# Last image: variance of the residual sum from a covariance gathered in the last attention, and residual sums made inside the q, k, v loop

## The chip, the cores and the metric

The kernel runs on one core of one Trainium2 chip. The metric is the device time of the whole program in microseconds (us): the median of several executions.

## The reference, cut to what matters

Four images of 256 channels and 64x64 pixels go through four residual layers. `N` is 4096 pixels; the 256 channels are held as two halves (`h` = 0, 1) of 128 partitions.

```
# layer 0: x + f(gn32(x)); f: 3x3 convolution, group norm, relu -> xs; then non-local attention on xs
f    = einsum('bnc,bcm->bnm', theta(xs), phi(xs))
attn = softmax(f, axis=-1)
y    = einsum('bnm,bmc->bnc', attn, g(xs))
w_y  = group_norm(conv1x1(y, w_w, w_b), gn2_w, gn2_b)
x    = x + (w_y * 0.1 + xs)
# layer 1: x + linear attention on gn(x); _gn takes mean and variance of groups of 8 channels
qkv  = einsum('oc,bchw->bohw', w_qkv, rmsnorm(gn(x)))
q, k = softmax over 32 channels, softmax over pixels
out  = rmsnorm(w_out @ (context(k, v) applied to q))
# layer 2: depthwise 3x3 and pointwise products with generated filters; layer 3: mixture of four 1x1 filters
```

Between layers 0 and 1 the kernel needs, for each channel, mean and variance over the pixels of the *residual sum* r = sc * wy + xin (+ a shift), where wy is the 1x1 convolution of the attention's result, sc its group-norm scale (known only when wy is complete), and xin the sum of x and xs.

## The kernel before, in words

Everything is fp32. The order of the instructions of each engine is that of the code (`manual_schedule`): a chain of generators (`Chain.steps`) is stepped together with the generator `attend`, and each `yield n` of the chain adds n times a rate to a credit; a whole unit of credit gives one turn to the attention. So while the attention of image b runs, the tail of image b-1 (`nonlocal_out`, `linear_attention`, `generated`, `mixed`) and the convolution of image b+1 fill the other engines. Images count from 0; the last is image 3, with `diag` and `xs_in` given in its tail. Its attention runs with the tail of image 2 beside it (rate 1.24) and then alone; its own tail runs after it, with nothing beside it except 16 pieces of image 2's last product, held back in `held`: `fill(n)` issues the matmuls of n pieces (4 matmuls of 512 columns each), `settle` drains them on VectorE and stores them.

- `attend(b)` (L888): 8 blocks `q` of 512 columns, each of 16 iterations `m`. An iteration makes two logits products (pf, L898), their exponentials on ScalarE (pr, L899), two products with g (py, L937), and adds pr into tot on VectorE. `ended` (L902) finishes a block in five stages, during the next block's first iterations: the sum inv (L906) at m=15; pss at m=0; the reciprocal and yt at m=1; ps_wy and its copies to wt (L922) at m=2; the statistics of wt (bn_stats, L925) and its store to DRAM (wy_d, L926) at m=3.
- `residual_sums` (L956): 16 passes of ScalarE over the last image's xin (`x_cols`), with a running sum, in the last block or so of the last attention. They give the mean of xin.
- `nonlocal_out` (L966): for the last image it loads wy six parts ahead (parts of 1024 columns and one half), closes the statistics of wy (`group_finish`, L330), makes sc and sh (`affine`, L365), adds sc * wy + xin into `big` in eight instructions of VectorE (L127), squares each around the known mean on ScalarE (L1014), and sums the squares (L1000, L1001).
- `group_finish`: a matmul pm averages the means over a group, VectorE makes ev, a matmul pv averages that, VectorE adds eps (rstd, L354), and POOL takes the power -1/2 (L217).
- `linear_attention` (L1023): `normed(c)` writes 512 columns, normalised, to xg (L1033) and their squares to sq (L1035) on ScalarE, and VectorE adds the halves of sq (s2; the profile calls it s). For each c: `normed(c+1)`; `qkv(c)`, 16 matmuls ps_qkv (L1057) with their evictions to qk (L1061) and v (L1062); the norms of c+1 (ps_ss, L1043, and rinv, L1045); `context(c-1)` (ps_qt, ps_ctx).
- Helpers: VectorE's `tt` is L124, `stt` L127.

Buffers: tiles of 4 KB a partition (pr, tot, wt, wy, xs, xg, sq, qk, v, z, dw, wp2, ex) share nine of one tag, `k4`; a new tile waits for the last reader of the one that had its place. The last tail takes every second of its tiles from four spare ones (`in_turns`), whose names in the profile are ra and rt.[...]

```python
def k4(name):
    return wk.tile([P, CH], F32, tag="k4", name=name, bufs=9)
```

Of the kernel before, what the change touches and what calls it, by code (L numbers as in the profile page):

```python
# [13 lines left out]
P = 128  # L14
# [79 lines left out]
def conv_preact_fast(ctx: ExitStack, tc: tile.TileContext, guard, x, wc, wtpg, ww, wqkv, wout, w1cat, wd2,  # L94
# [235 lines left out]
    def group_finish(st, avg, eps, shift=None):  # L330


        if callable(st):
            mv = st()
        else:
            mv = sp.tile([P, NH, 2], F32, name="mv")
            for h in range(NH):
                nc.vector.bn_aggr(mv[:, h, :], st[:, h, :, :].rearrange("p c s -> p (c s)"))
        if shift is not None:
            tt(mv[:, :, 0], mv[:, :, 0], shift, ALU.add)  # L340
        yield 1
        pm = bank("pm")
        nc.tensor.matmul(pm[:, 0:NH], avg, mv[:, :, 0], start=True, stop=True)
        gm = sp.tile([P, NH], F32, name="gm")
        nc.vector.tensor_copy(gm, pm[:, 0:NH])
        ev = sp.tile([P, NH], F32, name="ev")
        tt(ev, mv[:, :, 0], gm, ALU.subtract)
        tt(ev, ev, ev, ALU.mult)
        tt(ev, ev, mv[:, :, 1], ALU.add)
        yield 1  # L350
        pv = bank("pv")
        nc.tensor.matmul(pv[:, 0:NH], avg, ev, start=True, stop=True)
        rstd = sp.tile([P, NH], F32, name="rstd")
        nc.vector.tensor_scalar(rstd, pv[:, 0:NH], eps, None, ALU.add)  # L354
        rsqrt(rstd, rstd)
        return mv, gm, rstd
# [530 lines left out]

    def attend(b):  # L888

        probs, todo = {}, []  # L890
        st = wy_stats[b] = sp.tile([P, NH, 8, 6], F32, name="wy_st")

        def logits(i):
            q, m = divmod(i, NM)
            pr = k4("pr")
            for s in range(2):
                pf = bank("pf")
                nc.tensor.matmul(pf, phi[:, bass.ts(2 * m + s, P)], theta[:, bass.ts(q, 512)], start=True, stop=True)  # L898
                nc.scalar.activation(pr[:, bass.ts(s, 512)], pf, AF.Exp)  # L899
            probs[i] = pr  # L900

        def ended(q, py, tot):  # L902

            at = b * NQ + q
            inv = wk.tile([P, 512], F32, tag="inv", name="inv")
            nc.vector.scalar_tensor_tensor(inv, tot[:, 0:512], 1.0, tot[:, 512:CH], ALU.mult, ALU.add,  # L906
                                           accum_out=guard[:, 0, at:at + 1])
            yield
            pss = bank("pss")
            nc.tensor.matmul(pss, ones, inv, start=True, stop=True)  # L910
            yield
            nc.vector.reciprocal(inv, pss)  # L912
            yt = k2("yt")
            tt(yt, py, inv, ALU.mult)
            yield
            nc.scalar.activation(junk(), inv, AF.Copy, accum_out=guard[:, 1, at:at + 1])

            wt = k4("wt").rearrange("p (h n) -> p h n", h=NH)
            for h in range(NH):
                ps = bank("ps_wy")  # L920
                nc.tensor.matmul(ps, ww_s[:, bass.ts(h, P)], yt, start=True, stop=True)  # L921
                nc.scalar.copy(wt[:, h, :], ps)  # L922
            yield
            for h in range(NH):
                nc.vector.bn_stats(st[:, h, q, :], wt[:, h, :])  # L925
            nc.sync.dma_start(out=wy_d[b].rearrange("h p n -> p h n")[:, :, bass.ts(q, 512)], in_=wt)  # L926

        logits(0)
        for i in range(NQ * NM):
            q, m = divmod(i, NM)  # L930
            if m == 0:
                py = bank("py")
                tot = k4("tot")
            if i + 1 < NQ * NM:
                logits(i + 1)
            for s in range(2):
                nc.tensor.matmul(py, g[:, bass.ts(2 * m + s, P)], probs[i][:, bass.ts(s, 512)],  # L937
                                 start=(m == 0 and s == 0), stop=(m == NM - 1 and s == 1))
            if m == 1:
                tt(tot, probs[i - 1], probs[i], ALU.add)  # L940
            elif m > 1:
                tt(tot, tot, probs[i], ALU.add)
            for t in todo:
                next(t, None)
            if m == NM - 1:
                todo = [ended(q, py, tot)]
                next(todo[0])
            yield i + 1 < NQ * NM
        for t in todo:
            for _ in t:  # L950
                yield


    res_sum = cp.tile([P, NH], F32, name="res_sum")

    def residual_sums(xs_in):  # L956

        parts = sp.tile([P, NH, N // 512], F32, name="res_parts", bufs=1)
        for h in range(NH):
            for c in range(N // 512):  # L960
                nc.scalar.activation(junk(), xs_in[:, h, bass.ts(c, 512)], AF.Copy, accum_out=parts[:, h, c:c + 1])
                yield
        nc.vector.tensor_reduce(res_sum, parts, AX.X, ALU.add)


    def nonlocal_out(w, b, big, k4, xs_in):  # L966
# [4 lines left out]
        def load_parts(i):  # L971
            c, h = PARTS[i]
            wy = k4("wy")
# [7 lines left out]
        ahead = 2 if xs_in is None else 6  # L981
        parts = [load_parts(i) for i in range(ahead)]
        if xs_in is not None:
            yield 1
        bias = vec_s[:, V_WB, :]
        wmv, gm, rstd = yield from group_finish(wy_stats[b], avg32, 1e-5, bias)
        sc, sh = affine(gm, rstd, vec_s[:, V_G2W, :], vec_s[:, V_G2B, :], bias, 0.1)
        st = stats_tile()
        if xs_in is not None:

            mv = sp.tile([P, NH, 2], F32, name="mv_in", bufs=1)
            centre = sp.tile([P, NH], F32, name="centre", bufs=1)
            squares = sp.tile([P, NH, N // CH], F32, name="squares", bufs=1)
            tt(mv[:, :, 0], wmv[:, :, 0], bias, ALU.subtract)
            tt(mv[:, :, 0], mv[:, :, 0], sc, ALU.mult)
            stt(mv[:, :, 0], res_sum, 1.0 / N, mv[:, :, 0], ALU.mult, ALU.add)
            nc.vector.tensor_scalar(centre, mv[:, :, 0], -1.0, None, ALU.mult)

            def moments():
                nc.vector.tensor_reduce(mv[:, :, 1], squares, AX.X, ALU.add)  # L1000
                nc.vector.tensor_scalar(mv[:, :, 1], mv[:, :, 1], 1.0 / N, None, ALU.mult)  # L1001
                return mv

            st = moments
        w.fill(2)
        for i, (c, h) in enumerate(PARTS):
            cols = bass.ts(c, CH)
            wy, xs = parts[i]
            stt(big[:, h, cols], wy, sc[:, h:h + 1], xs, ALU.mult, ALU.add)
            if i + ahead < len(PARTS):  # L1010
                parts.append(load_parts(i + ahead))
            yield 0.6
            if xs_in is not None:
                nc.scalar.activation(wy, big[:, h, cols], AF.Square, bias=centre[:, h:h + 1], accum_out=squares[:, h, c:c + 1])  # L1014
            else:
                for s in range(2):
                    nc.vector.bn_stats(st[:, h, 2 * c + s, :], big[:, h, bass.ts(2 * c + s, 512)])
            yield 0.6
        w.settle()
        return st, sh  # L1020


    def linear_attention(w, b, big, qT, k4, st, sh, alone):  # L1023
        _, gm, rstd = yield from group_finish(st, avg8, 1e-5, sh)
# [56 lines left out]

        ahead = normed(0)
        yield 1
        ready = *ahead, None
        last = None
        for c in range(NC):
            if c + 1 < NC:
                ahead = normed(c + 1)
# [10 lines left out]
        rk = sp.tile([P, 1], F32, name="rk")  # L1099
# [98 lines left out]
    def generated(w, b, big, k4, st, sh, diag):  # L1198
        mv, gm, rstd = yield from group_finish(st, avg8, 1e-5, sh)

        pivot = sp.tile([P, NH], F32, name="pivot")
# [7 lines left out]
        hs = sp.tile([HT * HP, NC3], F32, name="hs")  # L1209
# [6 lines left out]
        b1n = sp.tile([HT * HP, 1], F32, name="b1n")  # L1216
# [33 lines left out]
        pooled = sp.tile([HT * HP, 1], F32, name="pooled")  # L1250
        nc.vector.tensor_reduce(pooled, hs, AX.X, ALU.add)
        pd = sp.tile([HT * HP, 2 * R], F32, name="pd")
# [5 lines left out]
        pb = sp.tile([P, 2 * R], F32, name="pb")  # L1258
# [3 lines left out]
        dk = sp.tile([P, NH * 9], F32, name="dk")  # L1262
# [118 lines left out]
        sh2 = sp.tile([P, NH], F32, name="sh2")  # L1381
# [4 lines left out]
    def mixed(w, b, big, k4, st, sh, held):  # L1386
# [7 lines left out]
        pool = sp.tile([P, NH], F32, name="rpool")  # L1394
# [6 lines left out]
        hid = sp.tile([EH, 1], F32, name="hid")  # L1401
# [6 lines left out]
        nm = sp.tile([P, 1], F32, name="lnm")  # L1408
        nc.vector.tensor_reduce(nm, pl[:, 0:NE], AX.X, ALU.max, negate=True)
        al = sp.tile([P, NE], F32, name="al")  # L1410
        asum = sp.tile([P, 1], F32, name="asum")
# [5 lines left out]
        scales = sp.tile([P, NH, NE], F32, name="scales")  # L1417
# [15 lines left out]
        b3 = sp.tile([P, NH], F32, name="b3")  # L1433
# [46 lines left out]
    def tail(b, big, qT, k4=k4, diag=None, xs_in=None, held=None):  # L1480

        def layers(w):
            st, sh = yield from nonlocal_out(w, b, big, k4, xs_in)
            st = yield from linear_attention(w, b, big, qT, k4, st, sh, diag is not None)
# [33 lines left out]
    with tc.manual_schedule(engines={E.PE, E.Activation, E.DVE, E.Pool, E.SP}):  # L1518
# [20 lines left out]
        sums = residual_sums(x_cols)  # L1539
        while next(attention, False):  # L1540
            for _ in range(3):
                next(sums, None)
        for _ in sums:
            pass
# [592 lines left out]
```

## Time and profile before

| | |
|---|---|
| median of three runs | 3113.34 us (3112.62 to 3114.3) |
| the profiled execution: its time | 3113.69 us |
| the profiled execution: its span | 3111.8 us |
| TensorE matmul, weight load | 3006.8 us (97%), 1486.8 us (48%) |
| VectorE, ScalarE, POOL | 2109.5 us (68%), 1174.0 us (38%), 131.1 us (4%) |
| last attention | first logits 2244.75 us, last py ends about 2820 us |
| last image's q, k, v loop | first ps_qkv 2849.33 us |
| mean granted clock of TensorE | 0.989 |

Times in the profile are from the start of the span. A line of the timeline has start, duration, engine, line of the kernel, operation, out<-in, shape and count; in brackets the idle time of the engine ahead of it and what ended it. A line of a table by stretch has the stretch, its length, then for PE (matmuls), PEld (weight loads), DVE (VectorE), ACT (ScalarE) and POOL the busy time and the number of instructions, then the granted clock, the busy share of the DMA engines and GB/s. Ends of matmuls are modelled.

### The profile page before, as it was taken

The numbers are of one execution on the slowest core, as the hardware profiler recorded it, in microseconds if no ns is written. First come the engines' busy times: TensorE is split into PE (matmuls) and PEld (weight loads), VectorE is DVE, ScalarE is ACT, GpSimd is POOL, SyncE is SP. The second block draws the span as 40 slices with busy tenths as digits, with TensorE's granted clock in tenths as the row PEclk, the third lists the DMA queues.
The fourth block names the chain that finished last, engine by engine and source line by source line (L and its number), as shares of the span: only waits on it lengthen the run. The fifth ranks groups of instructions, "written<-read, shape, count | busy, mean of one in ns | idle before, by whom it ended". The sixth has DMA issues, their size and how long they took to land.

```text
span 3111.8 us, 24418 instructions
## 1 busy us (share of the span) xinstructions
PE 3006.8 (97%) x8606; PEld 1486.8 (48%) x8606; DVE 2109.5 (68%) x2713; ACT 1174.0 (38%) x2188; POOL 131.1 (4%) x178
## 2 busy tenths in 40 slices
PE   6899999999999999999999999999999999998888
PEld 3454555445554444444565444444545544444633
DVE  8747777853557986786537896778363668864485
ACT  2134333353555322223364532222445443335621
POOL 0100000000110000000011000000100100000100
PEclk9999999999999999999999999999999999998999
DMA  5233111022101023113300102310420010111011
GB/s 217 77 105 137 35 51 30 31 55 85 40 11 34 7 75 125 39 43 63 109 11 1 41 21 82 107 46 29 102 75 1 11 34 14 44 49 63 14 61 65
DMA packets 58913, 174.25 MB, mean 56 GB/s; under 512 B 6432, under 2 KB 16416, under 8 KB 54560
## 3 DMA queue, kind: packets, MB, share of 16 engines
q1 hardware_dynamic: 54752, 155.85, 14.5%
q0 software_dynamic: 4032, 16.78, 2.9%
q8 instruction: 70, 1.15, 0.2%
q14 instruction: 59, 0.48, 0.1%
HBM read 111.26 MB, written 78.12 MB: 61 GB/s over the span
## 4 chain that ended last, share of the span: by engine, by line
PE 76%; DVE 17%; issue 5%; ACT 1%; DMA 0%; POOL 0%; POOLq 0%; SPq 0%; DVEq 0%; ACTq 0%
PE pf L898 22%; PE py L937 22%; PE ps_qkv L1057 5%; PE ps_conv L499 4%; DVE dw L127 4%; PE ps_tp L874 4%; PE ps_ex L1444 3%; DVE tot L124 3%; PE ps_pw L1298 3%; PE ps_conv L571 2%; PE ps_g L879 2%; PE ps_wy L921 2%; PE ps_o L1125 1%; DVE big L127 1%; DVE ra L127 1%
## 5 line engine op out<-in xcount | busy, mean ns | idle before, releaser
L899 ACT ACTIVATE pr<-pf 128x512 f32<-128x512 f32 x1024 | 603.6, 596 | 1183.8 <-PE pf L898 1138.1
L898 PE MATMUL pf<-tpg 128*128 128x512 f32 x2048 | 968.2, 595 | 2.9 <-ACT pr L899 2.9
L937 PE MATMUL py<-pr,tpg 128*128 128x512 f32 x2048 | 962.3, 592 | 2.5 <-ACT pr L899 2.3
L124 DVE TENSOR_TENSOR tot<-tot,pr 128x1024 f32<-128x1024 f32 x448 | 546.1, 1219 | 181.1 <-ACT pr L899 179.7
L937 PEld LDWEIGHTS py<-pr,tpg 128*128 128x128 f32 x2048 | 388.6, 190 | 494.4 <-issue 476.4
L898 PEld LDWEIGHTS pf<-tpg 128*128 128x128 f32 x2048 | 381.8, 190 | 438.4 <-issue 412.8
L127 DVE SCALAR_TENSOR_TENSOR dw<-xp,dk,dw 128x1008 f32<-128x1008 f32 x216 | 272.9, 1267 | 6.8 <-ACT dw L1290 3.7
L499 PE MATMUL ps_conv<-v,u 128*128 128x512 f32 x384 | 171.0, 593 | 3.6 <-DVE v L124 3.6
L1057 PE MATMUL ps_qkv<-wqkv_s,xg 128*128 128x384 f32 x384 | 129.9, 487 | 0.0
L124 DVE TENSOR_TENSOR tpg<-ps_g,bg_s 128x512 f32<-128x512 f32 x32 | 22.1, 691 | 144.4 <-PE ps_g L879 144.4
L874 PE MATMUL ps_tp<-big,wtpg_s 128*128 128x512 f32 x256 | 116.8, 599 | 3.0 <-ACT big L671 3.0
L499 PEld LDWEIGHTS ps_conv<-v,u 128*128 128x128 f32 x384 | 72.6, 190 | 96.5 <-issue 89.8
L217 POOL TENSOR_TENSOR rstd<-rstd,half 128x2 f32<-128x2 f32 x24 | 16.8, 701 | 2370.2 <-DVE rstd L354 2238.0
L1298 PE MATMUL ps_pw<-dw,pk 128*128 128x512 f32 x224 | 103.7, 597 | 8.7 <-DVE dw L127 8.7
L912 DVE RECIPROCAL inv<-pss 128x512 f32<-128x512 f32 x32 | 107.2, 3351 | 7.1 <-PE pss L910 7.1
L1057 PEld LDWEIGHTS ps_qkv<-wqkv_s,xg 128*128 128x128 f32 x384 | 72.2, 190 | 53.6 <-issue 9.3
L1067 DVE TENSOR_REDUCE qs<-qk 128x16 f32<-128x512 f32 x24 | 16.5, 686 | 118.6 <-ACT qk L1061 118.6
L875 ACT ACTIVATE tpg<-ps_tp,btp_s 128x512 f32<-128x512 f32 x64 | 43.7, 686 | 118.5 <-PE ps_tp L874 118.5
L874 PEld LDWEIGHTS ps_tp<-big,wtpg_s 128*128 128x128 f32 x256 | 47.5, 193 | 54.3 <-issue 49.8
L1127 ACT ACTIVATE junk<-ps_o 128x256 f32<-128x256 f32 x128 | 49.2, 385 | 63.7 <-PE ps_o L1125 59.4
L1298 PEld LDWEIGHTS ps_pw<-dw,pk 128*128 128x128 f32 x224 | 42.8, 192 | 63.1 <-issue 51.5
L1061 ACT ACTIVATE qk<-ps_qkv,rinv 128x256 f32<-128x256 f32 x96 | 45.5, 474 | 72.4 <-PE ps_qkv L1057 61.6
(339 smaller groups left out, 3147.2 us busy)
## 6 DMA issues: line engine op xcount, KB each, us to landing
xp<-in_x_dram SPq DMA_DIRECT2D x16, 1024.0 KB, 6.4
wy_d<-wt SPq DMA_DIRECT2D x32, 512.0 KB, 3.0
out_dram<-res SPq DMA_DIRECT2D x64, 256.0 KB, 2.0
wy<-wy_d SPq DMA_DIRECT2D x28, 512.0 KB, 4.6
xs_d<-big POOLq DMA_DIRECT2D x24, 512.0 KB, 11.0
u<-filters SPq DMA_DIRECT2D x48, 256.0 KB, 2.5
xs<-xs_d SPq DMA_DIRECT2D x24, 512.0 KB, 5.4
u<-rows_d SPq DMA_DIRECT2D x36, 256.0 KB, 3.1
```

The costliest lines, as they stand in the source:

```text
L124: nc.vector.tensor_tensor(o, a, b, op)
L127: nc.vector.scalar_tensor_tensor(o, a, s, b, op0, op1)
L499: nc.tensor.matmul(ps[oh], u(oh, h), v[:, bass.ts(h, 512)], start=(h == 0), stop=(h == NH - 1))
L571: nc.tensor.matmul(ps[:, bass.ts(oh, IY * IX)], u[i][:, h, bass.ts(oh, P)], v[:, i, bass.ts(h, IY * IX)], start=(h == 0), stop=(h == NH - 1))
L874: nc.tensor.matmul(ps, wtpg_s[:, h, k, :], big[:, h, cols], start=(h == 0), stop=(h == NH - 1))
L898: nc.tensor.matmul(pf, phi[:, bass.ts(2 * m + s, P)], theta[:, bass.ts(q, 512)], start=True, stop=True)
L899: nc.scalar.activation(pr[:, bass.ts(s, 512)], pf, AF.Exp)
L912: nc.vector.reciprocal(inv, pss)
L937: nc.tensor.matmul(py, g[:, bass.ts(2 * m + s, P)], probs[i][:, bass.ts(s, 512)], start=(m == 0 and s == 0), stop=(m == NM - 1 and s == 1))
L1057: nc.tensor.matmul(ps[:, 0:3 * HID], xg[:, h, bass.ts(j, P)], wqkv_s[:, h, :], start=(h == 0), stop=(h == NH - 1))
L1298: nc.tensor.matmul(ps, pk[:, h * NH * P + oh * P:h * NH * P + (oh + 1) * P], dw[h][:, bass.ts(s, 512)], start=(h == 0), stop=(h == NH - 1))
L1444: nc.tensor.matmul(ps, wm[h][:, bass.ts(oh, P)], big[:, h, bass.ts(c, 512)], start=(h == 0), stop=(h == NH - 1))
```

## The change

The last image's variance of r is put together from three parts: var(wy), which the attention gathers already; var(xin); and their covariance. In the last attention a block's xin (`xc`, 512 columns of both halves) is loaded from DRAM at m=2 into a k4 tile, its statistics are taken at m=6 and 8, and once the block's wt is there two instructions multiply (wt - pivot) by xc with a running sum into `joint`. The last block's two multiplies run inside `group_finish`. Mean and variance of r then follow from small steps on [128, 2] tiles, before r itself is made. The adds that make r are a generator, `on_the_way`: parts 0 and 1 run inside the second `group_finish` (after ev, ahead of pv's use), parts 2 and 3 at c=1 of the q, k, v loop, 4 and 5 at c=3, 6 and 7 at c=5; the loads of wy stand between. ScalarE's sums of xin and its squares around the mean fall away. Of the two held pieces that were issued together, one is issued after affine, one ahead of `normed(0)`, and both are drained after `normed(0)`. Some small tiles get one buffer instead of two.

```diff
-    def group_finish(st, avg, eps, shift=None):
+    def group_finish(st, avg, eps, shift=None, between=()):
...
         tt(ev, ev, mv[:, :, 1], ALU.add)
+        for f in between[0:1]:
+            f()
         yield 1
         pv = bank("pv")
...
         rsqrt(rstd, rstd)
+        for f in between[1:]:
+            f()
         return mv, gm, rstd
...
+        def multiply(q, h, wt, xc):
+            nc.vector.scalar_tensor_tensor(xc[:, h, :], wt[:, h, :], pivot_in[:, h:h + 1], xc[:, h, :], ALU.add, ALU.mult,
+                                           accum_out=joint[:, h, q:q + 1])
+
+        def with_residual(q, wt, xc):
+
+            if q == 0:
+                mv = sp.tile([P, NH, 2], F32, name="mv")
+                for h in range(NH):
+                    nc.vector.bn_aggr(mv[:, h, :], st[:, h, 0, :])
+                nc.vector.tensor_scalar(pivot_in, mv[:, :, 0], -1.0, None, ALU.mult)
+            if q < NQ - 1:
+                for h in range(NH):
+                    multiply(q, h, wt, xc)
+            else:
+                last_block.extend(lambda h=h: multiply(q, h, wt, xc) for h in range(NH))
...
             nc.sync.dma_start(out=wy_d[b].rearrange("h p n -> p h n")[:, :, bass.ts(q, 512)], in_=wt)
-
+            if b == B - 1:
+                with_residual(q, wt, xc)
...
+            if b == B - 1 and m == 2:
+                xc = k4("xc").rearrange("p (h n) -> p h n", h=NH)
+                nc.sync.dma_start(out=xc, in_=xs_d[b].rearrange("h p n -> p h n")[:, :, bass.ts(q, 512)])
+            if b == B - 1 and m in (6, 8):
+                h = m // 2 - 3
+                nc.vector.bn_stats(res_st[:, h, q, :], xc[:, h, :])
             for t in todo:
                 next(t, None)
             if m == NM - 1:
-                todo = [ended(q, py, tot)]
+                todo = [ended(q, py, tot, xc)]
...
-    def residual_sums(xs_in):
...
-                nc.scalar.activation(junk(), xs_in[:, h, bass.ts(c, 512)], AF.Copy, accum_out=parts[:, h, c:c + 1])
...
-            wy = k4("wy")
+            wy = (k4 if xs_in is None else pool4)("wy")
...
-        ahead = 2 if xs_in is None else 6
-        parts = [load_parts(i) for i in range(ahead)]
+        parts = [load_parts(i) for i in range(2)]
...
+            between = last_block
+        wmv, gm, rstd = yield from group_finish(wy_stats[b], avg32, 1e-5, bias, between)
...
+            tt(mv[:, :, 0], wmv[:, :, 0], bias, ALU.subtract)
+            tt(off, mv[:, :, 0], pivot_in, ALU.add)
+            for h in range(NH):
+                nc.vector.bn_aggr(rmv[:, h, :], res_st[:, h, :, :].rearrange("p c s -> p (c s)"))
+            nc.vector.tensor_reduce(cov, joint, AX.X, ALU.add)
+            tt(off, off, rmv[:, :, 0], ALU.mult)
+            stt(cov, cov, 1.0 / N, off, ALU.mult, ALU.subtract)
         sc, sh = affine(gm, rstd, vec_s[:, V_G2W, :], vec_s[:, V_G2B, :], bias, 0.1)
...
+            w.fill(1)
             tt(mv[:, :, 0], mv[:, :, 0], sc, ALU.mult)
+            tt(mv[:, :, 0], mv[:, :, 0], rmv[:, :, 0], ALU.add)
+            tt(mv[:, :, 1], wmv[:, :, 1], sc, ALU.mult)
+            stt(mv[:, :, 1], cov, 2.0, mv[:, :, 1], ALU.mult, ALU.add)
+            tt(mv[:, :, 1], mv[:, :, 1], sc, ALU.mult)
+            tt(mv[:, :, 1], mv[:, :, 1], rmv[:, :, 1], ALU.add)
+
+            def on_the_way():
+
+                for c in range(N // CH):
+                    for h in range(NH):
+                        added(2 * c + h, sc)
+                    yield
+                    if c + 1 < N // CH:
+                        parts.extend(load_parts(2 * c + 2 + h) for h in range(NH))
+                    yield
+
+            return (lambda: mv), sh, on_the_way()
         w.fill(2)
...
-                nc.scalar.activation(wy, big[:, h, cols], AF.Square, bias=centre[:, h:h + 1], accum_out=squares[:, h, c:c + 1])
...
+        alone = sums is not None
+        _, gm, rstd = yield from group_finish(st, avg8, 1e-5, sh, (lambda: next(sums),) if alone else ())
...
+        if alone:
+            w.fill(1)
+            next(sums)
         ahead = normed(0)
+        w.settle()
         yield 1
         ready = *ahead, None
         last = None
         for c in range(NC):
+            if alone and c > 0:
+                next(sums, None)
             if c + 1 < NC:
                 ahead = normed(c + 1)
...
-        sums = residual_sums(x_cols)
         while next(attention, False):
-            for _ in range(3):
-                next(sums, None)
-        for _ in sums:
             pass
```

`added(i, sc)` is the add that stood in the loop of `nonlocal_out`: `stt(big[:, h, cols], wy, sc[:, h:h + 1], xs, ALU.mult, ALU.add)`.

## The prediction

> **What bounds the kernel now.** I read the page first, then TensorE's waits in the last attention, then tables by stretch, then the timeline where the last attention ends.
>
> ```profile
> PE 3006.8 (97%) x8606; PEld 1486.8 (48%) x8606; DVE 2109.5 (68%) x2713; ACT 1174.0 (38%) x2188; POOL 131.1 (4%) x178
> ```
>
> TensorE is the bound: from 2244 to 2820 us (last attention) the waits list shows no TensorE wait at all. The table by stretch (PE, PEld, DVE, ACT, POOL):
>
> ```profile
> 2560.00:2710.00 150.00, 150.00 (x350) 66.31 (x350) 127.24 (x121) 53.12 (x89) 0.00 (x0) 1.00 0.02 7
> 2753.00:2811.00 58.00, 58.00 (x149) 26.41 (x148) 30.70 (x51) 30.16 (x67) 0.70 (x1) 1.00 0.20 64
> ```
>
> PE is full in both, DVE at 85% in the first. What lies beside it costs nothing until it makes TensorE wait. TensorE does starve between attention and the last tail (timeline):
>
> ```profile
> 2828.56 0.58 DVE L338 BATCH_NORM_AGGREGATE mv<-wy_st 128x2 f32<-128x48 f32 x2
> 2831.05 6.61 PE L1444 MATMUL ps_ex<-big,wmh 128*128 128x512 f32 x8
> 2833.69 1.28 DVE L127 SCALAR_TENSOR_TENSOR tpg<-ra,sc,xp 128x1024 f32<-128x1024 f32 x1
> ...
> 2843.26 1.40 DVE L127 SCALAR_TENSOR_TENSOR res<-ps_ex,b,big 128x512 f32<-128x512 f32 x2
> 2845.13 0.58 PE L343 MATMUL pm<-mv_in,avg 128*128 128x2 f32 x2 [7.46 <-DVE mv_in L124]
> 2847.18 0.16 DVE L354 TENSOR_SCALAR rstd<-pv 128x2 f32<-128x2 f32 x1 [0.68 <-PE pv L352]
> 2849.33 2.93 PE L1057 MATMUL ps_qkv<-wqkv_s,ra 128*128 128x384 f32 x4 [2.19 <-ACT ra L1033]
> ```
>
> Eight adds on DVE (1.28 us each, 1.2 apart) and two drains come before the moments can go to TensorE at 2845.13. The chain of waits runs through them.
>
> [...] matmuls stop at 2827.3, the clock is 0.5 from about 2831. [...] work begins at 2849.33, full clock only about 2857.3. [...] pr at 2327.04 (below) starts behind the qk and v that precede it. [...]
>
> ```profile
> 2323.59 1.06 ACT L1035 ACTIVATE sq<-xg 128x1024 f32<-128x1024 f32 x1
> 2325.48 0.47 ACT L1061 ACTIVATE qk<-ps_qkv,rinv 128x256 f32<-128x256 f32 x1 [0.84 <-DVE s L124]
> ...
> 2327.04 1.09 ACT L899 ACTIVATE pr<-pf 128x512 f32<-128x512 f32 x2 [0.82 <-PE py L937]
> ```
>
> pr (exp of the logits) needs nothing of py; it waits 0.82 us for py because all nine k4 buffers are taken and the py before it, having read the older pr, frees one.
>
> **Step 1, the gap: -8.2 us.** Up to the third ev (2830.39) nothing changes. Then DVE: multiply h0 has no row; the nearest is inv L906, a 128x512 scalar_tensor_tensor with a sum, 0.69+0.08. I take 0.75 (ends 0.7 and 0.9). It ends at 2831.2, as pv does, so rstd stays at 2831.23; multiply h1 lies beside POOL's 0.70 and ends at 2832.05. Nine small steps follow (two tt, two aggregates of 0.58 together, reduce, two on the covariance) to 2833.3; affine's six take 0.73 as now, to 2834.06; six on mv and the shift, 0.08 where independent and 0.19 where chained, end at 2835.15. So pm at 2835.2 instead of 2845.1. The one held product before it (4 matmuls of 0.86 at half clock) starts at 2831.25 and is out by 2834.7. From pm to rstd is 2.05 us now; adds 0 and 1 stand in DVE ahead of rstd and make it 3.76 (2 x 1.2 from 2836.5, then rstd at 2838.97, against 2847.18). Gain 8.2; ends 7.5 and 8.9. rstd to ps_qkv is 2.15 as now: ps_qkv at 2841.1. The second held product (2837.25 + 3.44) ends before it. The eight ACT squares vanish, off the path.
>
> **Step 2, the clock: -1.2.** The second product works TensorE just before the loop, so the half-speed phase, now 8.0 us into the loop (2849.3 to 2857.3), would end some 4 us into it: at most (8.0-4.2)/2 = 1.9. I take 1.2, ends 0 and 1.9.
>
> **Step 3, six adds inside the q, k, v loop: +2.2.** Before, around the second round:
>
> ```profile
> 2860.29 1.51 ACT L1033 ACTIVATE rt<-tpg,nb,rstd 128x512 f32<-128x512 f32 x2
> 2861.79 0.15 DVE L1045 TENSOR_SCALAR rinv<-ps_ss 128x4 f32<-128x4 f32 x1
> 2862.92 0.69 DVE L124 TENSOR_TENSOR s<-sq 128x512 f32<-128x512 f32 x1 [0.98 <-ACT sq L1035]
> 2865.52 0.95 PE L1043 MATMUL ps_ss<-ones,s 128*128 128x1 f32 x8
> ```
>
> Adds 2 and 3 stand behind this rinv: 2861.94 to 2864.4. ACT's second xg starts at 2864.46, sq at 2865.23, s at 2866.32, so ps_ss at 2867.06 instead of 2865.52: TensorE waits 1.54. Behind xg on ACT the evictions of q, k, v move 3 us; the spare PSUM banks hold them. Rounds 3 and 5 have context work and 1.2 us more room: 0.33 each. Sum 2.2, ends 0.5 and 4. SP's six reloads (4.6 us to landing) are asked for a round earlier; POOL's rinv stands ahead of the adds. Settling the held product moves behind the first s on DVE, whose next s comes 2.5 us later: nothing.
>
> **Step 4, the last attention.** Added per block: two bn_stats (0.685, row wy_st) and two multiplies (0.75), 2.9 us of DVE, about 22 in all; DVE goes from 85% to 90% in its fullest stretch. Hidden; each us that it were late on tot would hold a pr buffer. The loads add 8 x 512 KB where the DMA engines are 2 to 20% busy (last column but one above). Removed: 16 ACT sums of 0.81 beside a full PE, worth nothing. The xc load has four iterations of 3.44 us until bn_stats; xs lands in 5.4. Late, it would stop tot behind it, then pr. It also stands on SP ahead of the store of wt. The bufs=1 tiles are used once an image: nothing.
>
> The buffer costs. [...]xc takes a k4 tile from m=2 of its block to m=3 of the next, so two live during m=2 to 3. In block 1 that is where image 2's q, k, v loop starts. Count in the order of the code when sq(2) (2323.59) is written: xg(1), xg(2), qk(0), v(0), pr, tot, wt: 7, sq the 8th. With two xc it is the 10th of nine. What frees a tile? pr needs tot and wt needs bn_stats, both behind s(2) on DVE, which waits for sq; qk(0) needs context behind ps_ss(2). Only xg(1), when TensorE ends its q, k, v at 2330.7. Then sq 2330.9, s to 2332.7, tot to 2333.9, then qk and v of round 1 free the PSUM bank that ps_ss(2) takes: 2334.8, not 2330.71. pr waits on for xc(0): wt's bn_stats to 2335.1, multiplies to 2336.65; ps_qt takes pr's bank at 2337.4, not 2331.5. Loss 5.9. Some 6 us of near-idle TensorE would bring half clock [...]: I take 2. Together +8.0; ends 0 and 11. Later rounds: one xc, 9 of 9 tiles, pr delayed 2 us into ACT's 3.8 us of slack a round: nothing.
>
> **Sum:** -8.2 -1.2 +2.2 +8.0 = +0.8. The profiled execution took 3113.69 (span 3111.8 and 1.9 around it); its median stands 0.35 lower at 3113.34. So 3114.1; own range 3109 to 3119.5.
>
> **Rivals.** *The tiles don't clash*: an xc is freed sooner than I count, step 4 costs 0 to 1. For it: TensorE never waits in this attention now. Against: the 0.82 us wait, which my count foretells. Clock and adds at their better values: -8.2 -1.5 +1.5 +0.5 = -7.7, 3105.6. *Slower: image 2's loop is short of a tile in every round*, because xc of the next block is loaded ahead. With seven tiles sq can wait for xg, which ends with TensorE's own 5.2 us of q, k, v; s then comes about 2 us late. Six further rounds: +12, 3126. Against: SP's loads get tiles in the order of the code: in SP's own waits the third xs of image 2 waits 25.7 us for a tot, though only six or so of the nine tiles hold anything then. It decides from three such rounds (+0.8 + 6 > 6.2).
>
> **Chances.** About 0.2% (6.2 us) is what a measurement can tell here. Forecast 0.42 (all within); no clash 0.32 (0.30 faster, 0.02 within); short every round 0.26 (0.25 slower, 0.01 within). Faster 0.30, within 0.45, slower 0.25. Range 3104.5 to 3124: it leaves out half of the slow rival and a little of the fast one.
>
> **What would show it.** Step 1: pm of the last tail about 10 us earlier and ps_qkv about 8 after the same start. Step 2: half clock over some 4 us into the loop. Step 3: ps_ss waiting 1.5, 0.3, 0.3. Step 4: TensorE waits at ps_ss and ps_qt in block 1 of the last attention, and none elsewhere in it. No such wait there, or waits in each round, proves me wrong.

## The result, and the profile after

The changed kernel takes 3120.45 us (median of 18 runs, 3118.26 to 3121.4), the kernel before 3114.44 us (18 runs, 3112.62 to 3116.05). The ratio is 1.0018, with a 95% interval from 1.0011 to 1.0025: 6 us more. That lies in the forecast range, 6.35 us above the forecast and 0.95 above the narrower range given for the sum alone (3109 to 3119.5). It is below the 0.2% that the prediction counts as no change, but the interval does not hold 1. The profiled execution took 3120.24 us, with a span of 3118.5 where it was 3111.8: +6.7, which the stages below add up to.

The shares of the engines, from the page of the changed kernel:

```profile
PE 3012.4 (97%) x8606; PEld 1488.1 (48%) x8606; DVE 2130.6 (68%) x2770; ACT 1153.8 (37%) x2140; POOL 134.6 (4%) x178
```

VectorE has 21 us more work, as counted, and ScalarE 20 less. The same two stretches of the last attention as before:

```profile
2560.00:2710.00 150.00, 150.00 (x351) 66.38 (x350) 133.46 (x135) 54.03 (x88) 0.00 (x0) 1.00 0.07 21
2753.00:2811.00 58.00, 58.00 (x149) 26.48 (x148) 35.15 (x61) 18.18 (x33) 0.70 (x1) 1.00 0.09 29
```

VectorE went from 127 to 133 us in the fullest stretch, and TensorE is as full as before: the added VectorE work is hidden. But the list of TensorE's waits in the last attention (2244 to 2826 us), which was empty, now has three lines (total, times, longest):

```profile
PE ps_ctx L1125 <- ACT pr L927: 2.3, 1, 2.3
PE ps_ss L1089 <- DVE s L124: 2.0, 1, 2.0
PE ps_qt L1122 <- ACT v L1108: 0.8, 1, 0.8
```

Each occurs once, in block 1. ScalarE's timeline there shows why:

```profile
2322.30 1.51 ACT L1079 ACTIVATE xg<-big,nb,rstd 128x512 f32<-128x512 f32 x2
2331.22 1.06 ACT L1081 ACTIVATE sq<-xg 128x1024 f32<-128x1024 f32 x1 [7.41 <-PE ps_qkv L1103]
...
2337.25 1.09 ACT L927 ACTIVATE pr<-pf 128x512 f32<-128x512 f32 x2 [2.29 <-DVE xc L905]
```

sq reads only xg, done at 2323.8. It starts 7.4 us later, when the matmuls that read the round's older xg end: it waited for a place among the nine k4 tiles. And pr waits for the multiply that reads xc. TensorE in the same stretch (the bracket is its idle time and what ended that):

```profile
2333.14 1.02 PE L1089 MATMUL ps_ss<-ones,s 128*128 128x1 f32 x8 [2.02 <-DVE s L124]
2335.01 0.67 PE L1122 MATMUL ps_qt<-ident,qk 128*128 128x128 f32 x4 [0.85 <-ACT v L1108]
2337.99 2.06 PE L1125 MATMUL ps_ctx<-v,qk 128*128 128x129 f32 x8 [2.31 <-ACT pr L927]
2339.84 3.14 PE L926 MATMUL pf<-tpg 128*128 128x512 f32 x4
```

After 5.2 us of waits, ps_ctx and pf run at about half speed (1.06 and 1.88 us when the clock is full); the granted clock is 0.50 from 2335.5 to 2342.4 us. In the gap after the attention (all engines, lines left out at each "..."):

```profile
2836.77 0.58 DVE L339 BATCH_NORM_AGGREGATE mv<-wy_st 128x2 f32<-128x48 f32 x2
...
2839.07 1.96 PE L1496 MATMUL ps_ex<-big,wmh 128*128 128x512 f32 x4
...
2843.13 0.38 PE L344 MATMUL pm<-mv_in,avg 128*128 128x2 f32 x2 [2.10 <-DVE mv_in L124]
...
2844.21 2.47 DVE L127 SCALAR_TENSOR_TENSOR tpg<-wy,sc,xp 128x1024 f32<-128x1024 f32 x2
...
2846.60 0.15 DVE L357 TENSOR_SCALAR rstd<-pv 128x2 f32<-128x2 f32 x1
...
2848.69 1.65 PE L1103 MATMUL ps_qkv<-wqkv_s,ra 128*128 128x384 f32 x2
```

From the aggregate to pm is 6.4 us where it was 16.6. The first held product takes 1.96 us, and the granted clock is 1.00 there. The kernel before had already lost it: its clock is at half from 2830.1 us, 2.9 us behind the end of its last ps_wy (the prediction reads "about 2831"). In the changed kernel it stays full for 8.6 us, to 2844.1; the last section has what the profiles show of that. In the loop itself, round 1 (TensorE):

```profile
2856.88 5.41 PE L1103 MATMUL ps_qkv<-wqkv_s,ra 128*128 128x384 f32 x16
2864.18 1.46 PE L1089 MATMUL ps_ss<-ones,s 128*128 128x1 f32 x8 [1.89 <-DVE s L124]
...
2868.11 6.97 PE L1103 MATMUL ps_qkv<-wqkv_s,rt 128*128 128x384 f32 x16
```

The 16 matmuls after the wait take 6.97 us instead of 5.3. Last, the depthwise stage, TensorE of the kernel before and then of the changed one:

```profile
2977.38 20.55 PE L1339 MATMUL ps_dw<-xp,tpg 128*128 128x512 f32 x48
...
3007.50 2.07 PE L1298 MATMUL ps_pw<-dw,pk 128*128 128x512 f32 x2 [8.72 <-DVE dw L127]
```

```profile
2980.41 18.86 PE L1391 MATMUL ps_dw<-xp,tpg 128*128 128x512 f32 x44
...
3009.70 2.07 PE L1350 MATMUL ps_pw<-dw,pk 128*128 128x512 f32 x2 [9.22 <-DVE dw L127]
```

The change does not touch this stage, yet four records (two instructions) of ps_dw that stood ahead of the 9 us wait now stand behind it.

Lengths of stages, in us, each from the start of one TensorE instruction to the start of the next (profiled executions; the first column is a time):

| kernel | last ps_wy at | to first ps_qkv (gap) | to ps_cm (loop) | to first ps_dw | to ps_pw after its wait | to pm of the fourth layer | to ps_log | to count |
|---|---|---|---|---|---|---|---|---|
| before | 2825.31 | 24.02 | 65.84 | 62.21 | 30.12 | 57.09 | 4.26 | 36.66 |
| changed | 2833.52 | 15.17 | 69.51 | 62.21 | 29.29 | 59.86 | 4.43 | 37.66 |
| xc apart | 2826.02 | 15.49 | 67.85 | 62.13 | 29.42 | 59.35 | 4.43 | 37.40 |
| only xc(0) apart | 2825.58 | 15.17 | 68.21 | 62.17 | 29.43 | 59.71 | 4.44 | 37.57 |
| adds earlier | 2833.15 | 15.18 | 63.09 | 62.23 | 29.39 | 59.56 | 4.44 | 37.50 |
| product in the wait | 2833.48 | 15.18 | 66.05 | 62.17 | 28.49 | 60.28 | 4.24 | 36.24 |
| fraction back | 2833.74 | 15.64 | 69.51 | 62.21 | 29.57 | 57.67 | 4.07 | 37.04 |
| before, fraction moved | 2826.28 | 23.83 | 66.51 | 62.22 | 29.55 | 59.72 | 4.44 | 37.58 |
| adds first | 2835.14 | 22.70 | 66.22 | 62.22 | 29.47 | 59.61 | 4.44 | 37.53 |
| three edits | 2825.76 | 15.17 | 65.60 | 62.14 | 29.77 | 57.20 | 4.27 | 36.71 |
| three edits, later | 2841.81 | 15.76 | 63.09 | 62.19 | 29.65 | 57.33 | 4.21 | 36.80 |
| three edits, gap filled | 2825.05 | 17.61 | 65.56 | 62.30 | 28.26 | 57.85 | 4.06 | 35.42 |
| three edits, dw wait filled | 2826.34 | 15.18 | 65.60 | 62.16 | 29.08 | 57.53 | 4.06 | 35.26 |

Changed against before: last attention +8.2, gap -8.85, loop +3.7, from ps_dw to count +3.1, behind count +0.6: +6.7.

### The profile page after: what moved, and what is told of

Its sections match the earlier page's. It is cut to its first block, busy times and chain, and to the rows that moved or that the text cites. A ratio compares the mean times of both kernels' runs of the same rounds, so it can differ in the third digit from the quotient of the medians.

```text
span 3118.5 us, 24452 instructions
## 1 busy us (share of the span) xinstructions
PE 3012.4 (97%) x8606; PEld 1488.1 (48%) x8606; DVE 2130.6 (68%) x2770; ACT 1153.8 (37%) x2140; POOL 134.6 (4%) x178
## 4 chain that ended last, share of the span: by engine, by line
PE 75%; DVE 17%; issue 5%; ACT 2%; POOL 0%; DMA 0%; POOLq 0%; SPq 0%; DVEq 0%; ACTq 0%
PE pf L926 22%; PE py L968 22%; PE ps_qkv L1103 5%; PE ps_conv L504 4%; DVE dw L127 4%; PE ps_tp L879 4%; PE ps_ex L1496 3%; DVE tot L124 3%; PE ps_pw L1350 3%; PE ps_conv L576 2%; PE ps_g L884 2%; PE ps_wy L949 2%; PE ps_o L1177 1%; DVE big L127 1%; DVE ra L127 1%
```

## The experiments

My theory after the traces: four separate effects. The gap gains 8.9; the clash of two xc tiles loses 8; the adds lose about 6 in the loop, half of it by the clock; and a shift in the planner's account of steps, which nobody asked for, loses 3 in a stage that the change leaves alone. Rivals are given with each run. Each version was timed beside the kernel before, which then stood at 3114.15, 3115.22 or 3114.41 us; the ratios are to that. The changed kernel's 3120.45 was timed beside 3114.44, so a difference of two versions is good to about 1 us. The cuts of code leave out lines at each "...".

**xc apart.** ra and rt are idle in the last attention, so xc goes there:

```diff
-                xc = k4("xc").rearrange("p (h n) -> p h n", h=NH)
+                xc = spare[q % 4].rearrange("p (h n) -> p h n", h=NH)
...
```

> The changed kernel with one edit: in the last attention xc is taken from the four blocks of ra and rt, which nothing uses then, instead of from k4. All DVE work, loads and multiplies stay. Tile theory (with xc(0) and xc(1) both alive in block 1, sq(2) of image 2 waits for xg(1)): the waits at ps_ss, ps_qt and ps_ctx in block 1 of the last attention (2.0, 0.9 and 2.3 us) go, and with them the half clock after them (3 us): 8.2 us less than the changed kernel's 3120.4, so 3112.2 (3110.5 to 3114). Rival (the 2.9 us of added DVE work a block holds up tot, and so TensorE): no change, 3119 to 3121, and the three waits stay.

Measured: 3109.97 us (ratio to before 0.9987, 0.998 to 0.9994), 10.5 less than the changed kernel, and 0.5 below the range expected. The list of TensorE's waits from 2244 to 2820 us is empty again. The same two instructions of ScalarE:

```profile
2322.76 1.51 ACT L1081 ACTIVATE xg<-big,nb,rstd 128x512 f32<-128x512 f32 x2
2324.30 1.06 ACT L1083 ACTIVATE sq<-xg 128x1024 f32<-128x1024 f32 x1
```

sq follows xg at once, with all the added VectorE work still there. The tile theory stands and the VectorE rival falls. The last ps_wy stands 0.7 after that of before, and the xg above stands 0.7 after that of before as well (2322.04): the added work costs nothing in between. Of the gain over 8.2, 1.7 lies in the loop, where the half clock behind the first wait lasts 3.4 us (2858.2 to 2861.6) and not 6.83; the late stages give 0.6.

**Only xc(0) apart.** The same, with `(k4("xc") if q else spare[0])`.

> The changed kernel with one tile moved: only block 0's xc is taken from ra, the other seven stay in k4. Theory (the one clash is that of xc(0) with xc(1) in block 1, where image 2's q, k, v loop starts; later blocks have room): as with all eight moved, 3110 (3109 to 3112), and no TensorE wait in the last attention. Rival (every block's xc takes from the nine tiles, block 1 is only the worst): 3113 to 3118, with waits left in later blocks.

Measured: 3111.22 us (0.9988, 0.998 to 0.9997), and no wait in the last attention. One of eight tiles made the whole clash; later blocks have room.

**Adds earlier.** The pair of adds for the next round is written after s and rinv, inside `qkv`, in the even rounds; the loads go in the odd ones.

```diff
                 if rinv is None:
                     rinv = norms(s2)
+                if j == 0:
+                    between()
...
-            if alone and c > 0:
+            if alone and c % 2:
                 next(sums, None)
...
-            this = yield from qkv(*ready)
+            this = yield from qkv(*ready, lambda: alone and c % 2 == 0 and next(sums, None))
```

> The changed kernel with one edit: in the q, k, v loop of the last tail each pair of adds is written half a round to a round earlier, after the sum s of the next block instead of ahead of its xg. Theory (the add stands ahead of xg on ACT, so ps_ss waits 1.9 us in round 1, and the clock halves because of that wait): the four ps_ss waits (2.4 us in all) and the half clock in round 1 (3.4 us) go, 5.8 us less than the changed kernel: 3114.6 (3113 to 3116.5). Rival (the clock would halve there anyway, as an after-effect of the gap before the loop): only the waits go, 3118. Second rival (the adds now delay the sums of q on DVE, and so the context matmuls): 3119 to 3122.

Measured: 3113.91 us (0.9999, 0.9991 to 1.0008), 6.5 less than the changed kernel. No ps_ss wait is left in the loop, and it takes 63.1 us instead of 69.5. VectorE shows the room that was there all along: in the changed kernel it stood idle for 3.50 us ahead of this qs (first line), and with the adds earlier they lie in that time:

```profile
2857.22 0.69 DVE L1113 TENSOR_REDUCE qs<-rt 128x16 f32<-128x512 f32 x1 [3.50 <-ACT rt L1107]
```

```profile
2853.21 0.15 DVE L1091 TENSOR_SCALAR rinv<-ps_ss 128x4 f32<-128x4 f32 x1
2853.28 2.47 DVE L127 SCALAR_TENSOR_TENSOR tpg<-wy,sc,xp 128x1024 f32<-128x1024 f32 x2
2857.83 0.69 DVE L1115 TENSOR_REDUCE qs<-rt 128x16 f32<-128x512 f32 x1 [2.08 <-ACT rt L1109]
```

**Product in the wait.** The adds stay; TensorE gets work for the wait, which tells the wait from the clock.

```diff
+            if alone and c == 1:
+                w.fill(1)
             if c + 1 < NC:
                 ready = *ahead, norms(ahead[1])
```

> The changed kernel with one line more: in round 1 of the q, k, v loop of the last tail, TensorE gets one of the held products (4 matmuls, 1.7 us) ahead of ps_ss(2), that is inside its wait for s; the last three held products, between ps_log and the last products, are then two. The adds stay where they are. Theory (the half clock after that wait comes of the wait): the loop from its first ps_qkv to ps_cm takes 66.1 us instead of 69.5, the end 2 us less, 3120.4 - 3.4 - 2 = 3115 (3113.5 to 3116.5). Rival (the clock would halve there anyway, as an after-effect of the gap): the loop takes 69 to 69.5 and the whole 3118 to 3118.5.

Measured: 3113.99 us (0.9999, 0.999 to 1.0007), loop 66.05 us. With 1.7 us of work added, the loop is 3.5 us shorter, and of the wait 0.17 us is left. Stretches 2864 to 2868, of the changed kernel and then of this one (the third column from the end is the granted clock):

```profile
2864.00:2866.00 2.00, 1.82 (x11) 1.85 (x12) 0.45 (x2) 1.81 (x6) 0.00 (x0) 0.65 0.38 86
2866.00:2868.00 2.00, 2.00 (x11) 2.00 (x10) 1.29 (x4) 1.37 (x3) 0.56 (x1) 0.50 0.45 176
```

```profile
2864.00:2866.00 2.00, 1.85 (x17) 1.88 (x18) 0.47 (x2) 2.00 (x7) 0.00 (x0) 1.00 0.45 84
2866.00:2868.00 2.00, 2.00 (x11) 1.35 (x10) 1.24 (x4) 1.97 (x4) 0.61 (x1) 1.00 0.66 209
```

With the work in the wait the granted clock is 1.00 in both stretches, where it was 0.65 and 0.50: the half clock came of the wait, and the rival (an after-effect of the gap) falls.

**Fraction back.** Steps of the planner are sums of fractions. The kernel before counted 16 x 0.6 = 9.6 in the loop over the parts of the last tail; the change dropped that, and with it the 0.6 that was left over. Put back:

```diff
+            yield 0.6
             return (lambda: mv), sh, on_the_way()
```

> The changed kernel with one line more: a step of 0.6 is counted where the loop over the parts used to count 9.6, which puts the fraction in the planner's account back to what it was in the kernel before. TensorE's order in the depthwise and pointwise stage of the last tail is then that of before (24 more ps_dw of this stage are unchanged in number, four of them stand again ahead of the long wait for dw). Theory (the four ps_dw of 0.43 us that had moved behind the wait are what the late part costs, with half-speed matmuls behind the wait on top): 1.7 to 3.7 us less than the changed kernel, 3116.7 to 3118.7. Rival (VectorE's chain alone sets that stage; the order on TensorE is of no account): 3120.4, within 0.5.

Measured: 3117.0 us (1.001, 1.0002 to 1.0019), 3.5 less than the changed kernel. From ps_dw to count: 128.35 us (before 128.13, changed 131.24).

**Before, fraction moved.** The mirror image, in the kernel before: `yield 0.4` behind its loop over the parts.

> The kernel before with one line more: a step of 0.4 is counted after the loop over the parts in the last tail, so that the planner's account has the fraction that it has in the changed kernel. Nothing else is changed. TensorE's order in the depthwise and pointwise stage of the last tail is then that of the changed kernel. Theory (order in that stage costs 1.7 us by itself, up to 3.7 with the half clock): 3116 to 3118 beside 3114.4. Rival (the order is of no account; the late loss of the changed kernel is another phase of the clock): 3114.4, within 0.5.

Measured: 3117.66 us (1.0011, 1.0005 to 1.0018), 3.5 more than before; ps_dw to count 131.29 us. The same 3 us, made and unmade by a fraction of a step, in both kernels. In the table 2.1 of them lie in the stage itself (the four records, at 0.43 us, are 1.7), 0.2 ahead of ps_log, and 0.9 in the products behind it. The last is the clock: around ps_log it is at half for 6.83 us in the kernel before (3065.66 to 3072.49) and for 10.2 us here (3067.8 to 3078.0). In the six profiles with a table by stretch there, it is 6.8 us in the two with the order of before (before, fraction back) and about 10 in the four others (changed, xc apart, adds earlier and this one); no run takes that apart from the order.

**Adds first.** All eight adds before the loop, the covariance kept; six parts are loaded ahead, as in the kernel before.

```diff
-                for c in range(N // CH):
-                    for h in range(NH):
-                        added(2 * c + h, sc)
-                    yield
+                for i in range(len(PARTS)):
+                    added(i, sc)
+                    if i + 6 < len(PARTS):
+                        parts.append(load_parts(i + 6))
+                yield
+                yield
```

> The changed kernel with all eight adds where the first two stand, ahead of rstd in the gap (with six pairs of the stored product loaded ahead, as in the kernel before); the covariance stays, nothing is added inside the loop. Theory (taking the adds out of the gap is most of step 1; the covariance only makes that possible): rstd comes 6 x 1.2 = 7.2 us later, so last ps_wy to first ps_qkv takes 22.4 us instead of 15.2; the loop has no ps_ss waits and takes about 65.8 instead of 69.5; the whole 3120.45 + 7.2 - 3.7 = 3124 (3122 to 3125.5). Rival (the reduction and squares that the covariance replaced were most of it): the gap takes 16 to 19 us, the whole 3117.5 to 3120.5.

Measured: 3124.05 us (1.0031, 1.002 to 1.0042); gap 22.7, loop 66.2. The covariance by itself shortens the gap by 1.3 us (24.0 to 22.7). The other 7.5 come from what it allows: pm no longer waits for r, so six of eight adds may go elsewhere.

**Three edits together** (xc apart, adds earlier, fraction back):

> The three edits together: xc in the blocks of ra and rt, the adds half a round to a round earlier, the planner's fraction put back. Theory (three separate losses; only the half clock in round 1 of the loop, of which the first edit alone already took 1.7 us, is counted twice): 3120.45 less 10.5, 6.5 and 3.5, plus 1.7: 3101.7 (3099.5 to 3103.5), 0.4% below the kernel before. Rival (what one edit saves at a wait, the clock takes back at the next, so that the gains do not add up): 3105 to 3110.

Measured: 3104.84 us (0.9969, 0.9958 to 0.998), 0.31% below the kernel before, but 3.1 above the forecast and just under the 3105 at which the rival begins. The gains do not quite add up, as the rival says. The table says where: the loop takes 65.6 us, not the 63.1 of the adds alone. The first rounds, of the three edits and then of the next kernel:

```profile
2840.93 2.24 PE L1106 MATMUL ps_qkv<-wqkv_s,ra 128*128 128x384 f32 x4 [2.13 <-ACT ra L1082]
...
2845.18 5.81 PE L1106 MATMUL ps_qkv<-wqkv_s,ra 128*128 128x384 f32 x12
```

```profile
2857.57 2.50 PE L1106 MATMUL ps_qkv<-wqkv_s,ra 128*128 128x384 f32 x4
...
2861.00 4.12 PE L1106 MATMUL ps_qkv<-wqkv_s,ra 128*128 128x384 f32 x12
```

The twelve matmuls take 5.81 or 4.12 us. With the three edits the granted clock is 0.50 from 2842 to 2848 us; in the changed kernel, where the twelve take 4.12 us as well, it is 1.00 from 2852 on.

**Three edits, later.** Work is added that nothing reads:

```diff
+        pd = bank("ps_ex")
+        for i in range(18):
+            nc.tensor.matmul(pd, ones, wqkv_s[:, :, 0:256], start=True, stop=True)
         next(last)
```

> The kernel with the three edits, and 18 matmuls of 128x512 that nothing reads, put between the last attention and its closing steps: 18 x 0.43 = 7.7 us of added work, so that the gap starts at about the time at which it starts in the changed kernel. Its order is otherwise that of the three edits. Theory (in which stretch the clock halves depends on when the idle stretches of the gap fall, and the changed kernel's later start is what saved it 2.5 us in the loop): the loop from first ps_qkv to ps_cm takes 63.1 us, as with the early adds alone, instead of 65.6, and the whole 3104.8 + 7.7 - 2.5 = 3110. Rival (the waits in the last attention, not the time, made the difference): the loop takes 65.6, the whole 3112.5.

Measured: 3117.62 us (1.001, 1.0001 to 1.0018); loop 63.09. I had mis-sized the shift: each such instruction is two records of 0.43 us, so the gap starts 16 us later, not 8. With 15.5 us of added work the theory gives 3104.84 + 15.5 - 2.5 = 3117.8 and the rival (the waits in the attention made the difference) 3120.3, both 0.8 lower if put on the kernel before as timed beside this one. There is no wait in this attention, and the loop is the short one, as its first round already was with xc apart alone; so the waits fall as the cause. The start within the span does not decide it either, since the last section has two starts 0.3 us apart with different outcomes. What does is not shown: no run was built to set it.

**Three edits, gap filled.** Two products after affine in place of one (`w.fill(2)`).

> The three edits together and two held products instead of one after the steps of affine, in the gap ahead of pm; the last three held products of the kernel are then two. Theory (the idle time ahead of pm, over 2 us, is what halves the clock in the gap and at the start of the loop; 1.7 us of products there end as pm is due): the 3 us that the half speed costs in the second product and the first round go, and the end is 2 us shorter as well: 5 us below the kernel with the three edits, so 3096 to 3099. Rival (pm is held up behind the products and the clock halves all the same): the end's 2 us only, less up to 1.5 for pm: 3099 to 3102.

Measured: 3104.24 us (0.9963, 0.9949 to 0.9977). My theory failed here: the two products ran at half speed (6.56 us instead of 3.6) and held pm up, the gap grew by 2.4, and the loop stayed at 65.6. The clock had halved already, at 2829.8, behind ps_wy. From ps_dw on 2.4 us were gained, 1.3 of them at the end; the rival has the mechanism, but its 3099 to 3102 was missed too. The five times go from 3100.3 to 3104.7, and the profile (3104.26) is of a slower one, so a faster execution may have another pattern of the clock; that was not measured.

**Three edits, dw wait filled.** One of the last three products moves ahead of the first ps_pw.

```diff
+            if diag is not None and c == 0 and s == 0:
+                w.fill(1)
+                w.later(2, w.settle)
```

> The kernel with the three edits, and one of the three last held products moved up to stand ahead of the first ps_pw of the last tail, whose wait for dw is 8.4 us; it is settled two steps later. Theory (TensorE is idle there and the products at the end take longer than VectorE needs for wm): that wait shrinks by 1.7 us, the end from ps_log is 1.3 us shorter, and nothing else moves: 3104.8 - 1.3 = 3103.5 (3102.5 to 3104). Rival (its two drains of 0.7 us stand in VectorE's chain of taps, which sets that stage): the stage is 1.4 us longer, and the whole 3104.9.

Measured: 3102.35 us (0.9961, 0.9947 to 0.9974), 0.39% below the kernel before and the lowest median of this study, though not clear of the gap filled (0.9963). It is 12.1 us below the kernel before timed beside it, the three edits 10.4 below theirs: 1.7 gained, where 1.3 was forecast. The wait fell from 8.4 to 5.95 us, the stage's two parts add up to 86.6 instead of 87.0, and the end takes 35.3 instead of 36.7. The drains of VectorE cost nothing that shows.

## Why the prediction came out near, step by step

- **Step 1, the gap: -8.2, measured -8.85.** Right in mechanism and size. The multiply took 0.74 + 0.08 us, and the small steps behind it 1.2 (the prediction counts nine and lists seven; there are seven). pm came 10 us earlier against the start of the gap. "Adds first" shows the part that I had not separated: 1.3 is the covariance, the rest is adds that leave the path.
- **Step 2, the clock: -1.2, measured -2.75** (between the first and the second round of the loop the difference to before grows from -0.6 to -3.4 us). The direction was right; the size was outside my ends. Half speed ended 2.3 us into the loop (2850.95), not 4, and the second held product lay in it (3.76 us, where the first took 1.96). That is luck: the three edits show that it does not belong to the change, for with the same gap of 15.2 us they have 65.6 us of loop, as before.
- **Step 3, the adds in the loop: +2.2, measured +6.4.** The waits were right: 1.89, 0.24 and 0.25 against 1.54, 0.33 and 0.33. The failed term is one that I did not have: the half clock behind the first wait, 3.4 us, which "product in the wait" shows. I had reckoned with that after the wait in the attention and not after this one.
- **Step 4, the last attention: +8.0, measured +8.2** (0.3 of that stands before block 1). The count of nine tiles was right, and so was its place: sq(2) at 2331.2 (forecast 2330.9), freed by ps_qkv's reading of xg(1), and no other wait in that attention. The inner sizes were a little off: waits of 5.2 (5.9) and a half clock of about 2.8 (2, an estimate of mine). The last wait came at ps_ctx, not at ps_qt; why ps_ctx waits for pr stays open.
- **What the sum lacked: +3.1 from ps_dw to count.** I followed every instruction that the change moves, but not what the removed steps leave in the planner's account; that remainder decided where matmuls stand 130 us later. Another 0.6 behind count is not explained: two other profiles (adds earlier, fraction back) have the same 6.85 us there, the rest 6.3 to 6.5.
- **The rivals.** That the tiles do not clash, and that every round is short of a tile, are both excluded by the list of waits and by the two xc runs.

So the sum, +0.8, came near because the largest two terms were right; the 6 us that it missed are the clock behind a 1.9 us wait (with step 2 set against it, net 2.6) and the planner's remainder (3.1), the rest 0.6 behind count and small errors that nearly cancel. These took the time out of the sum's own range (3109 to 3119.5). It lies in the recorded range because that was widened for the slow rival, whose mechanism did not occur: that part is luck.

## What to carry to other kernels

Before a buffer of a shared ring is held longer, count the live tiles at each point in the order of the code: that count gave place and cost of the stall, and moving one tile of eight removed it. Price a wait on a TensorE at full clock as the wait plus a slow phase that may follow, which behind a wait of 1.9 us lasted 6.83 us in the changed kernel, where it cost 3.4, and 3.4 with xc apart, where it cost 1.7; and look for idle time on the adding engine half a round earlier. When a step is removed from a planner that counts fractions, compare the order of the instructions of every later stage, also of those that the change doesn't touch.

## What the runs showed of the hardware that was not expected

A wait of 1.9 us, with small matmuls behind it, was followed by 6.8 us of half speed in the changed kernel (2864.6 to 2871.4; as long with the fraction back, 3.4 us with xc apart). One of 1.46 us at the same place (only xc(0) apart) was not: ps_ctx behind it took 1.06 us.

Tables by stretch, taken in quarters of a microsecond, give the moments at which the clock changed. In the changed kernel (the third column from the end is the mean clock, so 0.74 means full speed for 0.12 us of the 0.25, and a change at 2844.12):

```profile
2844.00:2844.25 0.25, 0.00 (x0) 0.00 (x0) 0.21 (x3) 0.00 (x0) 0.00 (x0) 0.74 0.00 0
2850.75:2851.00 0.25, 0.25 (x2) 0.00 (x0) 0.25 (x1) 0.25 (x1) 0.00 (x0) 0.61 0.00 0
2864.50:2864.75 0.25, 0.25 (x4) 0.25 (x3) 0.00 (x0) 0.25 (x2) 0.00 (x0) 0.70 0.00 0
2871.25:2871.50 0.25, 0.25 (x2) 0.19 (x1) 0.00 (x0) 0.25 (x2) 0.00 (x0) 0.65 0.52 213
```

The changes lie at 2844.12, 2850.95, 2864.60 and 2871.43: 6.83, 13.65 and 6.83 us apart, or 2, 4 and 2 times 3.41. In the profiles of the changed kernel and of the kernel before (18 and 16 changes between 137 and 3080 us) every distance between two changes is a whole multiple of 3.413 us. From 2810 to 3098 us in these two, TensorE was busy for 0 to 1.75 us of the last 3.41 us ahead of each of the 12 falls, and for at least 3.28 us of those ahead of each of the 12 returns. Neither figure is a limit: in the changed kernel it was busy for 1.63 us from 2833.88 to 2837.29 and full speed went on, and from 2864.60 to 2868.01 its 3.41 us were filled by ps_ss, ps_qt and ps_ctx, small products, and half speed went on. The 3.41 us with the wait, in the changed kernel and then with only xc(0) apart (TensorE's busy time comes first behind the length):

```profile
2861.19:2864.60 3.41, 1.52 (x8) 0.80 (x7) 0.88 (x2) 3.15 (x7) 0.00 (x0) 1.00 0.00 0
2855.15:2858.56 3.41, 1.95 (x9) 0.97 (x7) 1.00 (x2) 3.03 (x7) 0.04 (x1) 1.00 0.00 0
```

Half speed followed the first, and not the second.

In the gap, the instructions on TensorE are the same in nine kernels. Half speed fell on them in three patterns. The middle column has the time from the start of the last ps_wy to the first fall of the clock behind it, as the tables by stretch give it (to about 0.1 us), in the five kernels for which there is such a table ("-" in the others):

| kernels | last ps_wy to the fall, us | first product, second product, twelve matmuls of the first round, us |
|---|---|---|
| changed; adds earlier; product in the wait | 10.6; 10.5; - | 1.96, 3.76, 4.12 |
| three edits, later; fraction back; xc apart | -; 4.2; 4.8 | 3.76, 3.7 to 3.8, 4.12 |
| only xc(0) apart; three edits; dw wait filled | -; 5.8; - | 3.5 to 3.7, 1.96, 5.8 |

The start within the span does not decide the pattern: three edits (2825.76), xc apart (2826.02) and dw wait filled (2826.34) start close together, and the middle one has another pattern. What decides it is not shown. Since each kernel has one profile, how often an execution gets which pattern stays open too. Such a difference is worth 2.5 us in the loop, as much as many an edit: a stage length from one profile is good to that only.
